# Keeping the row exponentials of half the queries in every step, in an eight-batch attention kernel on one Trainium2 core

## The chip, the cores and the metric

The kernel runs on one core of one Trainium2 chip. A core has five engines that work side by side, each through its own list of instructions in order: TensorE (PE in the profile) multiplies matrices, VectorE (DVE), ScalarE (ACT) and GpSimd (POOL) work on elements, and SyncE (SP) issues transfers. They meet only at semaphores. Sixteen DMA engines move the data that SP and POOL ask for. SBUF has 128 partitions; PSUM, into which TensorE writes, has eight banks of 128 x 512 float32.

The metric is device time in microseconds (us). The kernel before takes 692.85 us, the median of three runs (692.49 to 692.99).

## The reference

The inputs are `x` (8 batches, 512 rows, 512 features), a condition vector per batch, three 512 x 512 weights and three biases, all float32. What has to come out:

```python
def _L0_cond_ref(x, tokens, Wq, bq, Wk, bk, Wv, bv):
    Q = _split_heads(x @ Wq.T + bq)       # 16 heads of 32
    K = _split_heads(x @ Wk.T + bk)
    V = _split_heads(x @ Wv.T + bv)
    tQ = _split_heads(tokens @ Wq.T + bq) # one row per batch
    tK = _split_heads(tokens @ Wk.T + bk)
    cQ = Q + tQ
    cK = K + tK
    scores = jnp.einsum('bhqd,bhkd->bhqk', cQ, cK) / jnp.sqrt(jnp.float32(HEAD_DIM))
    attn = jax.nn.softmax(scores, axis=-1)
    out = jnp.einsum('bhqk,bhkd->bhqd', attn, V)
    return out.transpose(0, 2, 1, 3).reshape(B, S, D_MODEL)
...
x = x + _L0_cond_ref(x, cond_1024[:, None, :], ...)
```

## The kernel before

**Steps.** Eight batches times four groups of four heads make 32 units, t = 0 to 31 (`T = B * G`). The main loop runs t = 1 to 28; each turn is called a step here. A step has four items, i = 0 to 3. The order of the instructions of PE, ACT, DVE and POOL is the order in which the program writes them (`manual_schedule`, L214); SP's DMAs are issued in one queue, in the order in which the scheduler left them, which is nearly the program's.

**What one item does.** `row_max` (L552, L585, L594) makes the scores of 128 queries of the *next* unit against all 512 keys, four heads in four PSUM banks, and takes their maxima on VectorE. `denominators` (L641) runs the exponential over the same banks on ScalarE with the maximum as bias, and keeps the sums; this is the row form, with the query on the partition. The weighted sum with V needs the other form, with the key on the partition. There are two ways to get it.

- *Second scores* (`exponentials`, L693, L696, L707). The maxima are split into three bfloat16 parts on POOL (`split_max`, L655 to L658), turned by a DMA on SP (`turn_max`, L667, the tile `maxT`), and added to a second product of keys and queries: per item four matmuls from `maxT` and four head products of 512 columns, and then four exponentials of 128 x 512 on ScalarE into tiles `e`. The row exponentials themselves are thrown away (they are written back to PSUM).
- *Kept* (`BLOCKED`, t = 3, 7, ..., 27). The row exponentials of all 512 queries are written to SBUF (the tile `blocks`). VectorE turns them in blocks of 32 x 32 (`turn_blocks`, L605, eight of 128 x 1024), and then DMAs exchange the blocks between the four groups of 32 partitions (`swap_blocks`, L625): six pairs of groups, each in three moves (one side to a spare tile `between`, the other side across, the spare tile back), per half of the queries. That is 18 DMAs of 128 KB per half, 36 per unit; of the first half all are on SP, of the second half nine are on SP and nine on POOL. Move 1 waits for move 0 and move 2 for move 1.

**Items and projections.** The four items of a step carry, after the scores, `V` (`weighted`, L716: the weighted sum of unit t - 1, its normalisation on DVE and POOL, and four DMAs of the result on SP, L785) and the products of the next batch's projections of q, k and v, one half of a seven-product scheme per item (`first_products` or `other_products`). Their sums are done on VectorE, except for q and k in blocked steps (`first_by_others`), where ScalarE copies and POOL adds. In a step t that is itself blocked, no item has second scores.

**Other transfers on SP.** Per step four DMAs load the residual `xr` (L188, on which POOL adds the bias at L196), four store the result (L785), one turns `maxT` (L667), and, up to the step in which the last batch is loaded, four load a block of `x` (L170), which VectorE turns (`turn_x`, L351) for the projections of the batch after next.

**Eight banks.** `begin` and `released` (L132, L139) keep a list of banks in the order of their release: an item with second scores uses all eight, an item without uses four for scores and two for the product.

The lines that carry an item are these:

```python
            begin(w)
            if not blocks:
                exponentials(t, i)
            late_first = item in ("v" if blocks else "qkv") and t % 2 == 1
            hold = row_max(*rows, late_first, w)
```

Of the kernel before, what the change touches and what calls it, by code (L numbers as in the profile page):

```python
# [17 lines left out]
def kernel(  # L18
# [38 lines left out]
    nc = tc.nc  # L57
# [13 lines left out]
    BLOCKED = [t for t in range(3, T - 4, G)]  # L71
# [3 lines left out]
    xp = ctx.enter_context(tc.tile_pool(name="xp", bufs=3))  # L75
    xtp = ctx.enter_context(tc.tile_pool(name="xtp", bufs=2))
    qkp = ctx.enter_context(tc.tile_pool(name="qkp", bufs=3))
    ep = ctx.enter_context(tc.tile_pool(name="ep", bufs=10))
# [119 lines left out]
    EB = ctx.enter_context(tc.tile_pool(name="eb", bufs=1))  # L198

    def room(name):  # L200
        return EB.tile([P, HG, NS, HG, P], F32, tag="eb", name=name)

    early = room("early").rearrange("p g c h s -> p (g c) (h s)")
# [126 lines left out]
    def transpose_x(n, pt, leaves=nc.vector.tensor_copy):  # L330

        b, sc = divmod(n, NS)
        if b >= B:
            return
        if sc == 0:
            xT[b] = xtp.tile([P, NC, S], F32, tag="xT", name=f"xT_{b}")
        for cc in range(NC):
            nc.tensor.transpose(
                pt[:, cc * P : (cc + 1) * P], xs[n][:, cc * P : (cc + 1) * P], ident
            )  # L340
        leaves(xT[b][:, :, sc * P : (sc + 1) * P], pt.rearrange("p (c s) -> p c s", c=NC))
        if n:
            load_block(n + 3)

    def turn_x(n):
# [6 lines left out]
        to_load.append(n + 3)  # L352
# [136 lines left out]
    def first_by_others(n, b, u, dens, small, at):  # L489

        one_, two_ = banks(at), banks(at + 1)
        c1, c12, c2, c22 = parts_of(n, b, u)
        dens()
        product(n, b, u, 1, one_[:, :HS])
        product(n, b, u, 6, two_[:, HS:])
        small()
        product(n, b, u, 2, two_[:, :HS], (0,))
        product(n, b, u, 7, one_[:, HS:])
        m1 = c2[:, 0, :]
        nc.scalar.copy(m1, one_[:, :HS])  # L500
        if n == "v":
            nc.scalar.copy(c1[:, 0, :], two_[:, :HS])
            nc.scalar.copy(c12, two_[:, HS:])
            nc.scalar.copy(c22, one_[:, HS:])
        else:
            nc.scalar.copy(c1, halves(two_))
            add = tok[:, "qk".index(n), u * 2 + 1, b : b + 1]
            nc.scalar.activation(c22, one_[:, HS:], AF.Identity, bias=add)
        for o in (c1[:, 0, :], c12):
            nc.gpsimd.tensor_tensor(o, o, m1, ALU.add)  # L510
        nc.gpsimd.tensor_tensor(c22, c22, c12, ALU.add)

    def other_products(n, b, u, dens, small, at):
# [10 lines left out]
        nc.vector.tensor_tensor(c2, halves(one_), twice(c22), ALU.add)  # L524
# [5 lines left out]
    def project_pair(n, b, r, dens, small, at, held):  # L530

        if r % 2:
            held()
        if b >= B:
            dens()
            small()
        elif r % 2:
            other_products(n, b, r // 2, dens, small, at)
        else:
            first_products(n, b, r // 2, dens, small, at, 0, held)  # L540


# [55 lines left out]
    blocked = {}  # L598

    def turn_blocks(t, units):  # L600

        for n in units:
            pr = slice(n % NP * 2, n % NP * 2 + 2)
            e = blocked[t][:, :, n // NP, pr, :].rearrange("p g h s -> p g (h s)")
            nc.vector.transpose(e, e)  # L605

    APART = [(a, g) for a in range(HG) for g in range(a + 1, HG)]
    between = {}

    def swap_blocks(t, half, move):  # L610

        def part(a, g):
            e = blocked[t][a * BL : (a + 1) * BL, g, half * 2 : half * 2 + 2]
            return e.rearrange("p c h s -> p (c h s)")

        if move == 0:
            between[t, half] = [
                ep.tile([P, 2, S], F32, tag="e", name=f"between_{t}_{half}_{i}") for i in range(2)
            ]
        for n, (a, g) in enumerate(APART):  # L620
            at = (n + 2) % HG * BL
            kept = between[t, half][n // HG][at : at + BL].rearrange("p i s -> p (i s)")
            to, of = [(kept, part(a, g)), (part(a, g), part(g, a)), (part(g, a), kept)][move]
            queue = nc.gpsimd if half and n % 2 else nc.sync
            queue.dma_start(to, of)  # L625

    def denominators(t, qc, w=HG):

        if t >= T - 2:
            return  # L630
        for j in range(HG):
            if t in BLOCKED:
                if t not in blocked:
                    blocked[t] = room(f"blocks_{t}")
                to = blocked[t][:, :, qc, j, :].rearrange("p g (c e) -> p g c e", e=BL)
            else:
                to = banks(w + j)
            of = banks(w + j)
            if t in BLOCKED:
# [9 lines left out]
    def split_max(t, on=nc.gpsimd):  # L649

        if t >= T or t in BLOCKED:
            return
# [9 lines left out]
    def turn_max(t):  # L662

        if t >= T or t in BLOCKED:
            return
# [22 lines left out]
    def exponentials(t, kc, at=None):  # L688
# [14 lines left out]
        for pr in range(NP):  # L703
            e = ep.tile([P, 2, S], F32, tag="e", name=f"e_{t}_{kc}_{pr}")
            es[t, kc, pr] = e
# [3 lines left out]
    def times_v(t, kc, pt, chunks=range(NS)):  # L709
        b, g = divmod(t, G)  # L710
        for j in range(HG):
            if t in BLOCKED:
                e = blocked[t][:, :, :, j, kc * BL : (kc + 1) * BL].rearrange("p a c e -> p c a e")
            else:
                e = es[t, kc, j // 2][:, j % 2, :]
# [3 lines left out]
                e,  # L719
                start=(kc == chunks[0]),  # L720
                stop=(kc == chunks[-1]),
            )
# [41 lines left out]
    def weighted(t, pt, pd, between):  # L764
# [4 lines left out]
        for kc in range(NS):  # L769
            times_v(t, kc, pt)  # L770
            if kc == 0:
                spread_sums(apart, pd)
# [200 lines left out]
    def products(t, n, blocks, hold, dens, small):  # L973

        b, r = (t - 1) // G + 1, (t - 1) % G
        if r % 2:
            hold()
            other_products(n, b, r // 2, dens, small, (0, 3))
            released(1, 2, 4, 5, 6, 7, 0, 3)
        elif blocks and n == "v":  # L980
            first_products(n, b, r // 2, dens, small, 5, 4, hold)
            released(6, 7, 0, 1, 2, 3, 5, 4)
        elif blocks:
            hold()
            first_by_others(n, b, r // 2, dens, small, 4)
            released(6, 7, 0, 1, 2, 3, 5, 4)
        else:
            first_products(n, b, r // 2, dens, small, 1, 0, hold)
            released(2, 3, 4, 5, 6, 7, 1, 0)

    TURNED = [((1, 1), (0, 1), (0, 1), (0, 1)), ((0, 0), (0, 1), (0, 1), (0, 1))]
    turned = {}

    def turn_more(t, i, late):

        for u in (t, t + 1):
            if u in BLOCKED:
                n = turned.get(u, 0)
                turned[u] = n + TURNED[t + 1 - u][i][late]
                turn_blocks(u, range(n, turned[u]))  # L1000

    SWAPS = {
        (-1, 2): [(0, 0)],
        (-1, 3): [(0, 1), (0, 2)],
        (0, 3): [(1, 0)],
        (1, 0): [(1, 1)],
        (1, 1): [(1, 2)],
    }

    for t in range(1, T - 3):  # L1010
        b, r = divmod(t, G)
        blocks = t in BLOCKED
        w = 0 if blocks else HG
        items = ["q", "k", "v", "V"] if t - 1 in BLOCKED else ["V", "q", "k", "v"]
        for i, item in enumerate(items):
            rows = (t + 1, i + 1) if i < 3 else (t + 2, 0)
            begin(w)
            if not blocks:
                exponentials(t, i)
            late_first = item in ("v" if blocks else "qkv") and t % 2 == 1  # L1020
            hold = row_max(*rows, late_first, w)

            def held(i=i, hold=hold):
                hold()
                if i == 2:
                    split_max(t + 1)
                    turn_max(t + 1)

            dens = lambda: denominators(*rows, w)
            if item in "qkv":  # L1030
                products(t, item, blocks, held, dens, nothing)
            else:
                held()
                dens()
                if blocks:
                    weighted(t - 1, banks(4), banks(5), nothing)
                    released(6, 7, 0, 1, 2, 3, 5, 4)
                else:
                    weighted(t - 1, banks(0), banks(1), lambda: turn_more(t, i, 0))
                    released(2, 3, 1, 4, 5, 6, 7, 0)  # L1040
            if i == 0 and r == 0:
                turn_x(t + NC + 2)
                turn_x(t + NC + 3)
            if i == 0 and r == 1:
                combine_x(b + 1, 1, nc.gpsimd)
            if i == 1 and r == 0:
                combine_x(b + 1, 0, nc.gpsimd)
            if i == 2 and r == 1:
                turn_x(t + NC + 3)
                turn_x(t + NC + 4)  # L1050
            if i == 3:
                load_blocks()
            if i == 2:
                aparts[t] = masked(t)
            if i == 3:
                load_residual(t + 1)
            turn_more(t, i, 1)
            for u in (t - 1, t, t + 1):
                if u in BLOCKED and (t - u, i) in SWAPS:
                    for swap in SWAPS[t - u, i]:  # L1060
                        swap_blocks(u, *swap)
# [26 lines left out]
    def crossed(t, kc, qc, u=None):  # L1088
# [28 lines left out]
        for pr in (1, 0):  # L1117
            e = ep.tile([P, 2, S], F32, tag="e", name=f"e_{t}_{kc}_{pr}")
# [161 lines left out]
```

## Time and profile before

The profiled execution has a span of 694.0 us, 1.15 us over the median of the three runs, so its rows can be used as they stand.

| What | Value |
|---|---|
| Median of three runs | 692.85 us |
| Profiled execution: span | 694.0 us, 22170 instructions |
| TensorE busy | 677.7 us (98%), 8824 matmuls |
| VectorE busy | 563.5 us (81%) |
| ScalarE busy | 563.6 us (81%) |
| GpSimd busy | 263.9 us (38%) |
| Granted TensorE clock | 0.998 |
| DMA queue of SP and its share of the 16 DMA engines | 54.78 MB, 41.4% |

How to read it: a float32 matmul appears as two matmul records. PE is busy nearly all the time, but its records are pipelined and their ends are modelled, so what a piece of work costs on PE is best read from one start to the next start in the timeline. SP's issuing of DMAs does not count as busy time anywhere; it is seen only in the timeline of SP, where a row gives the start of the first of several equal DMAs, the time until the last of them was issued, and their number. "PEld" is the loading of weights, which overlaps PE.

### The profile page before, as it was taken

The page shows a single profiled execution, that of the slowest core. Times are in us where ns is not written, and L with a number is a line of the kernel's source. Part 1 is how long each engine was busy: PE and PEld are TensorE (multiplying, and loading weights), DVE is VectorE, ACT ScalarE, POOL GpSimd, SP SyncE. Part 2 cuts the span into 40 slices and gives each one's busy share as a digit, 9 for nine tenths or more (in the row PEclk, how much of TensorE's full clock was granted, in tenths as well). Part 3 has the DMA queues.
Part 4 walks back from the last instruction along what each step waited for, and adds up shares of the span by engine and source line. Part 5 has one row for each costly group of instructions (what it writes and reads, how often), then busy time and mean ns, then how long its engine had stood idle before and what let it go on. Part 6 is the DMA issues. An engine that isn't in the chain of part 4 may idle for free.

```text
span 694.0 us, 22170 instructions
## 1 busy us (share of the span) xinstructions
PE 677.7 (98%) x8824; PEld 312.5 (45%) x8824; DVE 563.5 (81%) x878; ACT 563.6 (81%) x1427; POOL 263.9 (38%) x378
## 2 busy tenths in 40 slices
PE   9999999989999999999999999999999999999996
PEld 7444444435445444444445444453544544444331
DVE  4798799857989679886999778996798967987686
ACT  2589887878889888798879888798888988888564
POOL 3722422444236242454315352254423624243361
PEclk9999999999999999999999999999999999999999
DMA  7623236644366443672455624564427622365211
GB/s 188 107 48 55 46 57 145 130 85 70 55 154 152 79 71 69 138 166 48 69 126 116 139 48 74 131 133 108 72 39 154 159 41 41 74 134 146 47 31 31
DMA packets 231674, 65.50 MB, mean 94 GB/s; under 512 B 221834, under 2 KB 222346, under 8 KB 231572
## 3 DMA queue, kind: packets, MB, share of 16 engines
q1 hardware_dynamic: 226788, 54.78, 41.4%
q0 software_dynamic: 3024, 8.26, 4.5%
q8 instruction: 69, 1.13, 0.7%
q10 hardware_dynamic: 1760, 1.05, 0.5%
q14 instruction: 33, 0.27, 0.1%
HBM read 19.75 MB, written 8.39 MB: 41 GB/s over the span
## 4 chain that ended last, share of the span: by engine, by line
PE 83%; DMA 5%; SPq 4%; POOL 4%; issue 2%; ACT 1%; DVE 1%; DVEq 0%; POOLq 0%; ACTq 0%
PE psum L441 35%; PE psum L716 15%; PE psum L585 14%; PE psum L696 10%; PE psum L693 4%; PE psum L384 2%; SPq L785 2%; SPq L188 2%; DMA xr<-in_x_dram 1%; POOL res L782 1%; DMA x<-in_x_dram 1%; POOL res L781 1%; DMA maxT<-split 1%; POOL xr L196 1%; ACT e L707 1%
## 5 line engine op out<-in xcount | busy, mean ns | idle before, releaser
L641 ACT ACTIVATE psum<-psum,nmax 128x512 f32<-128x512 f32 x368 | 244.7, 673 | 28.6 <-DVE nmax L552 21.1
L552 DVE TENSOR_REDUCE nmax<-psum 128x1 f32<-128x512 f32 x298 | 191.3, 683 | 79.1 <-PE psum L585 76.9
L707 ACT ACTIVATE e<-psum 128x512 f32<-128x512 f32 x376 | 194.2, 602 | 66.0 <-PE psum L696 62.5
L585 PE MATMUL psum<-kT,qT 32*128 32x512 f32 x1024 | 143.0, 605 | 0.0
L594 DVE TENSOR_REDUCE nmax<-psum 128x2 f32<-128x1024 f32 x101 | 122.5, 1214 | 1.3 <-PE psum L585 1.3
L781 POOL TENSOR_TENSOR res<-res,recs 128x512 f32<-128x512 f32 x30 | 31.4, 1048 | 174.2 <-DVE res L780 153.6
L696 PE MATMUL psum<-qT,kT 32*128 32x512 f32 x752 | 96.7, 587 | 0.0
L716 PE MATMUL psum<-e,v 128*32 128x512 f32 x800 | 95.3, 597 | 0.0
L196 POOL TENSOR_TENSOR xr<-xr,bvs 128x512 f32<-128x512 f32 x30 | 38.4, 1279 | 145.9 <-DMA xr<-in_x_dram 140.8
L585 PEld LDWEIGHTS psum<-kT,qT 32*128 32x128 f32 x1024 | 60.8, 182 | 52.7 <-issue 23.3
L641 ACT ACTIVATION_READ_ACCUMULATOR psum<-psum,nmax 128x1 f32 x368 | 78.8, 214 | 0.0
L641 ACT ACTIVATE blocks<-psum,nmax 128x512 f32<-128x512 f32 x112 | 76.2, 719 | 0.0
L605 DVE STREAM_TRANSPOSE blocks<-blocks 128x1024 f32<-128x1024 f32 x56 | 68.5, 1224 | 0.0
L441 PE MATMUL psum<-wc_v,xc 128*32 128x256 f32 x768 | 50.2, 379 | 0.0
L441 PE MATMUL psum<-xc,wc_q 128*32 128x256 f32 x720 | 47.1, 379 | 0.0
L441 PE MATMUL psum<-xc,wc_k 128*32 128x256 f32 x720 | 47.1, 379 | 0.0
L716 PEld LDWEIGHTS psum<-e,v 128*32 128x32 f32 x800 | 20.8, 110 | 51.4 <-issue 29.2
L693 PE MATMUL psum<-maxT,onesb 3*128 3x512 bf16 x376 | 37.1, 385 | 2.7 <-DMA maxT<-split 1.9
L782 POOL TENSOR_TENSOR res<-res,xr 128x512 f32<-128x512 f32 x30 | 38.5, 1283 | 2.4
L696 PEld LDWEIGHTS psum<-qT,kT 32*128 32x128 f32 x752 | 37.4, 185 | 1.7
L780 DVE STREAM_TRANSPOSE res<-psum 128x512 f32<-128x512 f32 x28 | 20.1, 717 | 22.0 <-PE psum L716 18.9
L441 PE MATMUL psum<-wT_v,xT 128*32 128x256 f32 x512 | 36.8, 382 | 0.0
(182 smaller groups left out, 895.6 us busy)
## 6 DMA issues: line engine op xcount, KB each, us to landing
between<-blocks SPq DMA_DIRECT2D x63, 128.0 KB, 2.4
blocks<-blocks SPq DMA_DIRECT2D x63, 128.0 KB, 2.4
blocks<-between SPq DMA_DIRECT2D x63, 128.0 KB, 2.9
out_dram<-res SPq DMA_DIRECT2D x122, 64.0 KB, 1.9
xr<-in_x_dram SPq DMA_DIRECT2D x120, 64.0 KB, 2.4
x<-in_x_dram SPq DMA_DIRECT2D x112, 64.0 KB, 2.7
between<-blocks POOLq DMA_DIRECT2D x21, 128.0 KB, 3.5
blocks<-blocks POOLq DMA_DIRECT2D x21, 128.0 KB, 3.2
```

The lines of the kernel that those rows point to most:

```text
L196: nc.gpsimd.tensor_tensor(xr[t], xr[t], bias, ALU.add)
L441: nc.tensor.matmul(pt[r], still[:, r], moving, start=(kc == kcs[0]), stop=(kc == kcs[-1]))
L552: nc.vector.tensor_reduce(nmax[t][:, qc, j : j + 1, 0], pt, AX.X, ALU.max, negate=True)
L585: nc.tensor.matmul(pt, qkT["q", t][r, qc * P : (qc + 1) * P], qkT["k", t][r, :], start=True, stop=True,)
L594: nc.vector.tensor_reduce(nmax[t][:, qc, pr * 2 : pr * 2 + 2, 0], pt, AX.X, ALU.max, negate=True)
L605: nc.vector.transpose(e, e)
L641: nc.scalar.activation(to, of, AF.Exp, bias=nmax[t][:, qc, j, :], accum_out=sums[t][:, qc, j, :],)
L693: nc.tensor.matmul(bank[j], onesb[r, :], maxT[t][r, :], start=True, stop=False)
L696: nc.tensor.matmul(bank[j], qkT["k", t][r, kc * P : (kc + 1) * P], qkT["q", t][r, :], start=False, stop=True,)
L707: nc.scalar.activation(e[:, i, :], bank[pr * 2 + i], AF.Exp)
L716: nc.tensor.matmul(pt[j * HD : (j + 1) * HD, :], vs[b % 2][:, kc, (g * HG + j) * HD : (g * HG + j + 1) * HD], e, start=(kc == chunks[0]), ...
L782: nc.gpsimd.tensor_tensor(y, y, xr.pop(t), ALU.add)
```

## The change

The change spreads the kept form over all of steps 3 to 27 and halves it. `KEPT = range(3, T - 4)` replaces `BLOCKED`: in each of these 25 units the row exponentials of the first two of the four query tiles (256 queries) are kept, turned by four transposes of VectorE, and exchanged by 18 DMAs, all on SP. The other 256 queries get second scores, in two bursts (`exponentials_of_rest`): a burst has four matmuls from `maxT` over 512 columns, eight head products of 256 columns, and four exponentials of 128 x 512; each is an item's worth. So the items 0 and 1 of such a step have no second scores, and the items 2 and 3 have one burst each. The weighted sum is done in two halves of 256 columns, first the half with second scores, then the kept half (`times_v_half`).

With it go other edits:

- All exponentials live in one tile `store` of the same size as the two pools before: three rooms for kept halves, used in turn, four places for the bursts, two for the exchange's spare tile.
- The first halves of the projections are all made by `first_by_others` (two copies of 128 x 512 on ScalarE, two adds on POOL); the second half of v is made by `other_by_others` (two copies on ScalarE, three adds on POOL). VectorE keeps the second halves of q and k. The order of the three projections in a step is given by `MADE`, and `V` is the second item ("PVPP") where the unit before is kept.
- `x` has two buffers in place of three, and one block is loaded per step in place of two every other step.
- The exchange of unit t + 1 is issued at the end of step t, after the load of the residual; that of unit 3 in step 3 after its first item.

```diff
-    BLOCKED = [t for t in range(3, T - 4, G)]
+    KEPT = range(3, T - 4)
+    KQ = NS // 2
...
-    xp = ctx.enter_context(tc.tile_pool(name="xp", bufs=3))
+    xp = ctx.enter_context(tc.tile_pool(name="xp", bufs=2))
...
+    store = EB.tile([P, 18, 2, S], F32, tag="eb", name="store")
+
+    def room(t):
+
+        at = t % 3 * 4
+        return store[:, at : at + 4].rearrange("p g c (h s) -> p g c h s", s=P)
...
+    def first_by_others(n, b, u, dens, at, last):
...
+        product(n, b, u, 1, one_[:, 0])
+        product(n, b, u, 7, one_[:, 1])
+        product(n, b, u, 6, two_[:, 1])
+        product(n, b, u, 2, two_[:, 0], (0,))
         dens()
...
+        nc.scalar.copy(c2, one_)
+        nc.scalar.copy(c1, two_)
+        last()
+        nc.gpsimd.tensor_tensor(c1, c1, twice(c2[:, 0, :]), ALU.add)
         nc.gpsimd.tensor_tensor(c22, c22, c12, ALU.add)
...
+    def other_by_others(n, b, u, dens, small, at):
...
+        nc.scalar.copy(m45, halves(one_))
+        nc.scalar.copy(m23, halves(two_))
+        nc.gpsimd.tensor_tensor(c12, m45[:, 1, :], c12, ALU.add)
+        nc.gpsimd.tensor_tensor(c2, m45, twice(c22), ALU.add)
+        nc.gpsimd.tensor_tensor(c1, m23, c1, ALU.add)
...
+    def turn_kept(t, n):
+
+        pr = slice(n % NP * 2, n % NP * 2 + 2)
+        e = kept[t][:, :, n // NP, pr, :].rearrange("p g h s -> p g (h s)")
+        nc.vector.transpose(e, e)
...
+    between = store[:, 16:18]
+
+    def swap_kept(t, move):
 
         def part(a, g):
-            e = blocked[t][a * BL : (a + 1) * BL, g, half * 2 : half * 2 + 2]
-            return e.rearrange("p c h s -> p (c h s)")
...
+            return kept[t][a * BL : (a + 1) * BL, g].rearrange("p c h s -> p (c h s)")
+
         for n, (a, g) in enumerate(APART):
             at = (n + 2) % HG * BL
...
-            queue = nc.gpsimd if half and n % 2 else nc.sync
-            queue.dma_start(to, of)
+            aside = between[at : at + BL, n // HG].rearrange("p i s -> p (i s)")
+            to, of = [(aside, part(a, g)), (part(a, g), part(g, a)), (part(g, a), aside)][move]
+            nc.sync.dma_start(to, of)
...
+    def exponentials_of_rest(t, half):
+
+        bank = [banks(i) for i in range(HG)]
+        rest = slice(KQ * P, S)
+        for j in range(HG):
+            r = slice(j * HD, j * HD + 3)
+            nc.tensor.matmul(
+                bank[j],
+                onesb[r, :],
+                maxT[t][r, rest].unsqueeze(1).broadcast_to([3, 2, HS]),
+                start=True,
+                stop=False,
+            )
+        for i in range(2):
+            kc = half * 2 + i
+            for j in range(HG):
+                r = slice(j * HD, (j + 1) * HD)
+                nc.tensor.matmul(
+                    bank[j][:, i * HS : (i + 1) * HS],
+                    qkT["k", t][r, kc * P : (kc + 1) * P],
+                    qkT["q", t][r, rest],
+                    start=False,
+                    stop=(i == 1),
+                )
+        for pr in range(NP):
+            e = es[t, half, pr] = store[:, 12 + half * 2 + pr]
+            for i in range(2):
+                nc.scalar.activation(e[:, i, :], bank[pr * 2 + i], AF.Exp)
...
+        if t in KEPT:
+            for kc in range(NS):
+                times_v_half(t, kc, 1, pt)
+            spread_sums(apart, pd)
+            for kc in range(NS):
+                times_v_half(t, kc, 0, pt)
...
+    def bursts(s, i):
+
+        if s not in KEPT:
+            return [(s, i)]
+        return [(s, i - 2)] if i >= 2 else []
+
+    TURNED = {(0, 1): 1, (1, 1): 1, (2, 0): 1, (3, 1): 1}
...
+        items = "PVPP" if t - 1 in KEPT else "VPPP"
...
             if i == 3:
                 load_residual(t + 1)
...
+            if i == 3 and t in KEPT and t + 1 in KEPT:
+                for move in range(3):
+                    swap_kept(t + 1, move)
+            if (t, i) == (KEPT[0], 0):
+                for move in range(3):
+                    swap_kept(t, move)
```

258 lines of the change are left out of this document (119 added, 139 removed).

## The prediction

> **What bounds the kernel now.** I read the page's busy times first, then the page's chain, then windows over steps 3 to 27, and last the timelines of PE and SP inside these steps.
>
> ```profile
> span 694.0 us, 22170 instructions
> PE 677.7 (98%) x8824; PEld 312.5 (45%) x8824; DVE 563.5 (81%) x878; ACT 563.6 (81%) x1427; POOL 263.9 (38%) x378
> ...
> PE 83%; DMA 5%; SPq 4%; POOL 4%; issue 2%; ACT 1%; DVE 1%; DVEq 0%; POOLq 0%; ACTq 0%
> ```
>
> ```profile
> 108.90:622.30 513.40, 506.68 (x6868) 230.79 (x6864) 427.45 (x656) 438.83 (x1132) 199.81 (x295) 1.00 0.50 101
> 193.70:211.10 17.40, 17.40 (x244) 7.40 (x240) 15.37 (x22) 13.81 (x40) 7.84 (x13) 1.00 0.67 143
> 211.10:232.80 21.70, 21.70 (x300) 10.34 (x300) 17.91 (x29) 19.89 (x52) 9.41 (x17) 1.00 0.66 149
> ```
>
> The windows' columns are length, busy us of PE, PEld, DVE, ACT and POOL, clock, DMA share, GB/s. The first row is steps 3 to 27: 513.4 us for 25 steps. The second is step 7 (kept), the third step 8. PE is busy throughout, and 83% of the chain is PE: TensorE bounds the kernel. The 9% of DMA and SPq in the chain are the first hint that transfers are not all hidden.
>
> What an item costs on PE is read from start to start:
>
> ```profile
> 193.75 1.14 PE L585 MATMUL psum<-kT,qT 32*128 32x512 f32 x8
> ...
> 198.45 1.14 PE L585 MATMUL psum<-kT,qT 32*128 32x512 f32 x8
> ...
> 202.68 1.14 PE L585 MATMUL psum<-kT,qT 32*128 32x512 f32 x8
> ...
> 204.64 1.05 PE L441 MATMUL psum<-xc,wc_k 128*32 128x256 f32 x16
> 205.50 0.61 PE L441 MATMUL psum<-xT,wT_k 128*32 128x256 f32 x8
> ...
> 206.91 1.14 PE L585 MATMUL psum<-kT,qT 32*128 32x512 f32 x8
> ...
> 211.37 1.03 PE L696 MATMUL psum<-qT,kT 32*128 32x512 f32 x8
> 212.23 1.02 PE L585 MATMUL psum<-kT,qT 32*128 32x512 f32 x8
> ...
> 216.35 0.40 PE L693 MATMUL psum<-maxT,onesb 3*128 3x512 bf16 x4
> ...
> 221.56 0.39 PE L693 MATMUL psum<-maxT,onesb 3*128 3x512 bf16 x4
> ```
>
> A projection item without second scores takes 206.91 - 202.68 = 4.23 us, the V item without them 198.45 - 193.75 = 4.70, a projection item with them 221.56 - 216.35 = 5.21. A burst is worth 0.98. Four heads of 512 columns take 212.23 - 211.37 = 0.86; two groups of four with 256 columns take 205.50 - 204.64 = 0.86 as well, so halving the columns costs nothing by itself.
>
> Now SP, which counts as busy nowhere:
>
> ```profile
> 105.86 5.03 SPq L625 DMA_DIRECT2D between<-blocks  x6
> 110.99 3.70 SPq L625 DMA_DIRECT2D blocks<-blocks  x6
> 114.73 4.56 SPq L625 DMA_DIRECT2D blocks<-between  x6
> 119.39 2.19 SPq L785 DMA_DIRECT2D out_dram<-res  x4
> 122.95 1.21 SPq L667 DMA_TRANSPOSE maxT<-split  x1
> 124.21 3.74 SPq L188 DMA_DIRECT2D xr<-in_x_dram  x4
> ...
> 138.41 4.93 SPq L170 DMA_DIRECT2D x<-in_x_dram  x8
> ```
>
> ```profile
> 601.84 4.57 SPq L625 DMA_DIRECT2D between<-blocks  x6
> 606.72 3.69 SPq L625 DMA_DIRECT2D blocks<-blocks  x6
> 610.46 5.16 SPq L625 DMA_DIRECT2D blocks<-between  x6
> 615.72 2.21 SPq L785 DMA_DIRECT2D out_dram<-res  x4
> 618.95 2.10 SPq L667 DMA_TRANSPOSE maxT<-split  x1
> 621.09 2.17 SPq L188 DMA_DIRECT2D xr<-in_x_dram  x4
> ```
>
> These are the first and the last of seven exchanges of 18 DMAs, of exactly the size that the change issues in each of 25 steps. From the first issue to the end of the last they take 12.3 to 14.2 us, 13.1 in the mean, all of it SP's own time. The next rows say why some are longer:
>
> ```profile
> L625 SPq DMA_DIRECT2D between<-blocks x63: 507/589/2140, 105.9 to 625.7; - x63
> ...
> blocks<-between SPq DMA_DIRECT2D x63, 128.0 KB, 2.9
> ...
> maxT<-split SPq DMA_TRANSPOSE x22, 2.5
> ```
>
> The issue of one takes 0.59 us in the median and now and then 1.2 to 2.1. Such long issues fall about 9 us apart. The page's queue of instruction loads has 69 packets in the span, one per 10 us, and the long issues lie on those (packets at 106.5 and 116.5 us, long issues of the first exchange at 106.5 and 116.6):
>
> ```profile
> q8 instruction: 69, 1.13, 0.7%
> ```
>
> **The change part by part.** *TensorE.* Steps 3 to 27 had 18 x 4 = 72 bursts and get 50. By the items above 22 x 0.98 = 21.6 us go. The weighted sum in halves and the bursts in 256 columns cost 0 by the equal 0.86; its cover is that weights load beside the matmuls (7.40 us of PEld in 17.40), and if that were gone it would cost the difference between 1.05 (the row's own length) and 0.86 per pair of groups: 25 x 12 groups are 150 pairs, 0.19 x 150 = 28 us at most. I take 0, since the 256-column row is the nearest. A step then needs 4.23 + 4.70 + 2 x 5.21 = 19.35 us of PE, 25 steps 484. The 513.4 of before also hold waits: seven kept steps of 17.4 and 18 of 21.3 (3 x 5.21 + 5.68, V being 0.47 longer) make 505; 8 us are waits.
>
> *VectorE and ScalarE.*
>
> ```profile
> L605 DVE STREAM_TRANSPOSE blocks<-blocks 128x1024 f32<-128x1024 f32 x56 | 68.5, 1224 | 0.0
> ...
> L707 ACT ACTIVATE e<-psum 128x512 f32<-128x512 f32 x376 | 194.2, 602 | 66.0 <-PE psum L696 62.5
> ...
> L506 ACT COPY kT<-psum 128x512 f32<-128x512 f32 x7 | 4.2, 605 | 0.0
> L476 DVE COPY v<-psum 128x256 f32<-128x256 f32 x14 | 5.8, 414 | 0.0
> ```
>
> The transposes go from 56 to 100: +44 x 1.22 = +54 us on VectorE. It loses the first halves of the projections and v's second halves: 126 operations of 256 columns (0.41) and, net, 28 of 512 (about 0.6, half of 1.22 for 1024), 69 us. That leaves (427 + 54 - 69)/25 = 16.5 us a step, under 19.35. ScalarE loses 88 exponentials at 194.2/376 = 0.52 (-46) and gains 98 copies of 512 columns at up to 0.6 less 28 short ones of about 0.4 (+48): it stays near 438.8/25 = 17.6. POOL gains 70 adds of 512 columns (1.28 each, by a row below) and loses the issue of 63 DMAs: 199.8/25 = 8.0 a step become at most 11.6. All three stay under PE, and lie beside it. Costed at 0; if an item's ScalarE work runs over PE's (an item with a burst and two copies needs some 5.7 for 5.21), the cost is 0.5 x 25 = 12 us at most.
>
> *SP.* Here the cost stands. In each of steps 3 to 26 SP issues an exchange (13.1), a block of x (4.93/2 = 2.4), a result (2.2), maxT (1.3) and the residual (2.3, with 2.2 and 3.7 in the rows), with 0.1 between groups, 0.5 in all: 21.8 us. That is more than PE's 19.35, so SP falls behind by 2.4 us a step. Ends: without any long issue 3 x 3.69 + 2.2 + 1.2 + 2.2 + 2.4 and 0.4 between are 19.5; the first exchange with its neighbours adds up to 13.4 + 2.2 + 1.2 + 3.7 + 2.4 = 23.0. I take 21.8, from the mean of the seven, since the instruction loads go on and an SP that never rests meets every one.
>
> Who waits: all of it is one queue in order. The exchange is followed by x, the result, and then by maxT of the unit after, without which the bursts of that unit (L693) can't begin; behind maxT stands xr, on which POOL's adds wait (L196). The weighted sum's kept half waits for the last move, which lands 2.9 after its issue. What is late next is maxT, about 2 us per step. That such a wait reaches PE is seen once already, in step 4 behind two exchanges:
>
> ```profile
> 146.96 1.06 PE L716 MATMUL psum<-blocks,v 128*32 128x512 f32 x8 [1.75 <-DMA blocks<-between]
> ```
>
> *The sum*, along SP, to maxT of unit 28, which step 28 needs in its first item:
>
> ```profile
> 115.77 1.28 POOL L782 TENSOR_TENSOR res<-res,xr 128x512 f32<-128x512 f32 x1
> ...
> 622.32 0.40 PE L693 MATMUL psum<-maxT,onesb 3*128 3x512 bf16 x4
> ```
>
> In SP's order the result of unit 2 stands behind the first DMA of unit 3's exchange; it is ready at 115.8 + 1.3 = 117.1. From there 2.2 (result), 1.2 (rest of x), 12.4 (17 of the exchange) and 3.8 (maxT, xr): unit 4's exchange starts at 136.7. Units 4 to 22 are 19 x 21.8 = 414.2, units 23 to 26, with no x left, 4 x 19.4 = 77.6, and unit 27's exchange, a result and maxT to its landing 13.1 + 2.2 + 0.3 + 2.5 = 18.1: 646.6. Before, that burst started at 622.3. The rest is as before: 694.0 + 24.3 = 718.3, and, since the profiled execution stands 1.15 over the median, 717 us. PE, with 484 us from 108.9, would be there at 593.
>
> **The rivals.** *SP keeps up; TensorE decides (faster).* If a step's issues take 19.4 us or less, the 21.6 us of bursts go, and up to 8 us of waits: 663 to 671. For it: the last move of one exchange was issued while earlier ones were in flight, so 3.7 for six may be bound by data and not by issuing, and idle gaps could swallow the long issues. Against it: no exchange of the seven took less than 12.3. The Trainium skill has a rule that speaks for this rival: "DMA: Bandwidth & Descriptors", section "Issuing engines are not separate DMA queues", says that the sequencer's time to initiate a DMA is usually small relative to the DMA itself. By that page's fabric ceiling of 435 GB/s ("Where 436 GB/s comes from") a 128 KB move is an estimated 0.3 us, 18 of them 5.4, and a step on SP 14, so SP would have room. The trace differs: 0.59 of issue each, 18 in 12.3 or more.
>
> *Between.* A step on SP of 19.5 to 20.7: break-even is where 24.3/23 = 1.06 us a step are missing from 21.8, at 20.7. 664 to 691.
>
> *It waits on itself (slower still).* If PE's wait for the last move and SP's wait for PE's later items come one behind the other, the 1.75 above recurs in 25 steps, +44: 761. Against it: by the sum each thing that SP issues is ready by its turn (split of maxT some 6 us into an item that began with the last maxT).
>
> **How the numbers follow.** SP bounds the steps: 0.70, with 700 to 742 (21.0 to 22.9 a step). SP keeps up: 0.15. Between: 0.07. Within 0.2% of before, which is about what a measurement can tell here: 0.03. It waits on itself: 0.05. Faster 0.22, same 0.03, slower 0.75. The point is SP's, 717. The range leaves out the first rival and the last, 0.20: 680 (20.2 a step) to 742.
>
> **What would show it.** Right: SP's timeline has no gap from 120 to 640 us, and a step (from one first transpose of `store` to the next) takes about 21.8 us up to unit 22 and 19.4 to 20 after; PE is busy under 93%, with 40 us or more of waits on maxT and on the exchange. An exchange still takes 13 us. Wrong: gaps on SP in each step, steps of 19.4 (first rival), or steps of over 23 with SP waiting for semaphores (last). What would make the prediction wrong first is the 13.1: the same DMAs taking 11 or 15 us when one exchange follows another without a rest.

## The result, and the profile after

The changed kernel takes 728.01 us, the median of four runs (724.80 to 731.27), against 692.92 us before (four runs): a ratio of 1.048 with a 95% interval from 1.0427 to 1.0532. It is slower, by 35 us. Its profiled execution, the slowest of the four, took 731.27 us and has a span of 729.3 us. In all runs here the time of an execution is about 2 us (1.7 to 2.4) more than its span, so the 694.0 us of span before belong to an execution of an estimated 696 us, about 3 us over its median and not 1.15; below, spans are compared with spans.

The page of the kernel after (span, busy times, the chain, SP's largest group of DMAs):

```profile
span 729.3 us, 24078 instructions
PE 682.2 (94%) x9760; PEld 345.6 (47%) x9760; DVE 555.7 (76%) x740; ACT 564.3 (77%) x1409; POOL 335.1 (46%) x427
...
PE 68%; SPq 16%; DMA 5%; POOL 5%; DVE 3%; issue 2%; ACT 1%; DVEq 0%; POOLq 0%
...
store<-store SPq DMA_DIRECT2D x450, 128.0 KB, 2.4
```

The page's DMA queues (SP's is the first, the second loads instructions; packets, MB, share of the 16 engines):

```profile
q1 hardware_dynamic: 243124, 89.93, 60.8%
q8 instruction: 77, 1.26, 0.8%
```

TensorE's busy share falls from 98% to 94%, and SP's queue rises in the chain from 4% to 16%. The window over steps 3 to 27 of the kernel after, columns as in the prediction:

```profile
112.14:658.08 545.94, 505.72 (x7773) 260.44 (x7770) 429.54 (x544) 435.38 (x1106) 263.41 (x338) 0.97 0.72 149
```

These 25 steps took 513.4 us before and take 545.9 now: 32.5 of the 35.3 us by which the span grew. Of the 545.9, PE is idle for 40.2. VectorE and ScalarE have as much to do as before, POOL 64 us more, and all three have room. SP's timeline in the kernel after, at the first exchanges, at unit 23, and at the last one:

```profile
120.69 1.95 SPq L833 DMA_DIRECT2D out_dram<-res  x4
122.69 1.03 SPq L170 DMA_DIRECT2D x<-in_x_dram  x2
123.76 11.68 SPq L628 DMA_DIRECT2D store<-store  x17
135.48 2.42 SPq L668 DMA_TRANSPOSE maxT<-split  x1
137.94 2.18 SPq L188 DMA_DIRECT2D xr<-in_x_dram  x4
140.24 14.13 SPq L628 DMA_DIRECT2D store<-store  x18
154.42 2.23 SPq L170 DMA_DIRECT2D x<-in_x_dram  x4
156.76 2.04 SPq L833 DMA_DIRECT2D out_dram<-res  x4
158.90 2.40 SPq L668 DMA_TRANSPOSE maxT<-split  x1
161.35 2.17 SPq L188 DMA_DIRECT2D xr<-in_x_dram  x4
...
559.27 13.27 SPq L628 DMA_DIRECT2D store<-store  x18
...
638.77 14.36 SPq L628 DMA_DIRECT2D store<-store  x18
653.23 2.21 SPq L833 DMA_DIRECT2D out_dram<-res  x4
655.54 1.22 SPq L668 DMA_TRANSPOSE maxT<-split  x1
```

Each row of the first block begins where the one before it ends, within 0.12 us. From 120.7 to 659.0 us SP has no gap between two issues longer than 0.42 us. From unit 4's exchange to unit 23's there are 19 cycles in 419.0 us, 22.05 each; from unit 23's to unit 27's four in 79.5, 19.9 each. An exchange takes 12.9 us in the mean (11.3 to 14.4).

What PE waits for in the kernel after (us in total, times, longest), with the first row of another engine's waits that leads to it:

```profile
POOL xr L196 <- DMA xr<-in_x_dram: 152.0, 24, 9.8
PE psum L451 <- POOL xc L381: 24.7, 6, 4.9
PE psum L715 <- DMA maxT<-split: 12.5, 9, 3.0
PE psum L694 <- DMA maxT<-split: 2.3, 1, 2.3
```

The largest wait isn't on SP's transfers themselves. The timelines of POOL and PE, kernel after, step 5, show how it arises:

```profile
165.76 1.26 POOL L196 TENSOR_TENSOR xr<-xr,bvs 128x512 f32<-128x512 f32 x1 [9.31 <-DMA xr<-in_x_dram]
166.98 1.26 POOL L380 TENSOR_TENSOR xc<-xT 128x512 f32<-128x512 f32 x1
168.20 1.26 POOL L381 TENSOR_TENSOR xc<-xT,xc 128x512 f32<-128x512 f32 x1
```

```profile
162.53 0.40 PE L715 MATMUL psum<-maxT,onesb 3*128 3x512 bf16 x4 [1.64 <-DMA maxT<-split]
...
169.52 1.94 PE L451 MATMUL psum<-xc,wT_q 128*32 128x256 f32 x16 [4.87 <-POOL xc L381]
171.23 1.93 PE L451 MATMUL psum<-xc,wc_q 128*32 128x256 f32 x16
172.93 1.04 PE L451 MATMUL psum<-xT,wT_q 128*32 128x256 f32 x8
```

SP issues the residual late, POOL stands in order in front of its bias (L196) for 9.31 us, and behind it wait two adds (L380, L381) without which the next batch's projection can't begin. This occurs in every fourth step, six times.

### The profile page after: what moved, and what is told of

Same layout as the page of the kernel before. It is cut to its first block, busy times and chain, and to the rows that moved or that the text cites. A ratio compares the mean times of both kernels' runs of the same rounds, so it can differ in the third digit from the quotient of the medians.

```text
span 729.3 us, 24078 instructions
## 1 busy us (share of the span) xinstructions
PE 682.2 (94%) x9760; PEld 345.6 (47%) x9760; DVE 555.7 (76%) x740; ACT 564.3 (77%) x1409; POOL 335.1 (46%) x427
## 3 DMA queue, kind: packets, MB, share of 16 engines
q1 hardware_dynamic: 243124, 89.93, 60.8%
## 4 chain that ended last, share of the span: by engine, by line
PE 68%; SPq 16%; DMA 5%; POOL 5%; DVE 3%; issue 2%; ACT 1%; DVEq 0%; POOLq 0%
PE psum L451 31%; PE psum L595 14%; SPq L628 7%; PE psum L757 6%; PE psum L726 4%; PE psum L741 3%; SPq L833 3%; PE psum L697 3%; DMA xr<-in_x_dram 2%; SPq L188 2%; SPq L170 2%; PE psum L394 2%; SPq L668 2%; PE psum L715 1%; DMA maxT<-split 1%
## 5 line engine op out<-in xcount | busy, mean ns | idle before, releaser
L562 DVE TENSOR_REDUCE nmax<-psum 128x1 f32<-128x512 f32 x242 | 155.9, 686 | 102.6 <-PE psum L595 101.3
L642 ACT ACTIVATE psum<-psum,nmax 128x512 f32<-128x512 f32 x280 | 185.7, 670 | 17.9 <-DVE nmax L604 9.4
L736 ACT ACTIVATE store<-psum 128x512 f32<-128x512 f32 x200 | 103.3, 604 | 84.4 <-PE psum L726 84.4
L604 DVE TENSOR_REDUCE nmax<-psum 128x2 f32<-128x1024 f32 x129 | 156.7, 1215 | 2.8 <-PE psum L595 2.8
L642 ACT ACTIVATE store<-psum,nmax 128x512 f32<-128x512 f32 x200 | 136.2, 692 | 12.1 <-DVE nmax L604 7.1
L614 DVE STREAM_TRANSPOSE store<-store 128x1024 f32<-128x1024 f32 x100 | 122.5, 1226 | 0.0
L196 POOL TENSOR_TENSOR xr<-xr,bvs 128x512 f32<-128x512 f32 x30 | 38.3, 1275 | 163.2 <-DMA xr<-in_x_dram 152.0
L757 PE MATMUL psum<-store,v 128*32 128x256 f32 x1600 | 93.3, 381 | 0.0
L757 PEld LDWEIGHTS psum<-store,v 128*32 128x32 f32 x1600 | 46.9, 110 | 45.0 <-ACT store L642 17.4
L707 ACT ACTIVATE store<-psum 128x512 f32<-128x512 f32 x88 | 45.5, 608 | 14.8 <-PE psum L697 11.5
L726 PE MATMUL psum<-qT,kT 32*128 32x256 f32 x800 | 53.1, 382 | 0.0
L451 PE MATMUL psum<-xc,wT_q 128*32 128x256 f32 x240 | 20.3, 465 | 24.7 <-POOL xc L381 24.7
L642 ACT ACTIVATION_READ_ACCUMULATOR store<-psum,nmax 128x1 f32 x200 | 41.5, 207 | 0.0
```

The lines of the kernel that those rows point to most:

```text
L451: nc.tensor.matmul(pt[r], still[:, r], moving, start=(kc == kcs[0]), stop=(kc == kcs[-1]))
L562: nc.vector.tensor_reduce(nmax[t][:, qc, j : j + 1, 0], pt, AX.X, ALU.max, negate=True)
L604: nc.vector.tensor_reduce(nmax[t][:, qc, pr * 2 : pr * 2 + 2, 0], pt, AX.X, ALU.max, negate=True)
L642: nc.scalar.activation(to, of, AF.Exp, bias=nmax[t][:, qc, j, :], accum_out=sums[t][:, qc, j, :],)
L707: nc.scalar.activation(e[:, i, :], bank[pr * 2 + i], AF.Exp)
L726: nc.tensor.matmul(bank[j][:, i * HS : (i + 1) * HS], qkT["k", t][r, kc * P : (kc + 1) * P], qkT["q", t][r, rest], start=False, stop=(i == 1),
```

## The experiments

The prediction's theory is that SP's issuing bounds steps 3 to 27. The rivals after the result were the 16 DMA engines (their share is now 60.8% in SP's queue), POOL's place for the bias, and TensorE itself.

**Without the exchange.** SP's 18 DMAs go, so the kept half is weighted with blocks that were not exchanged; everything else stays.

```diff
-            if i == 3 and t in KEPT and t + 1 in KEPT:
-                for move in range(3):
-                    swap_kept(t + 1, move)
-            if (t, i) == (KEPT[0], 0):
-                for move in range(3):
-                    swap_kept(t, move)
```

> The changed kernel without the 18 exchange DMAs of each step (so the kept half is weighted with blocks that were turned but not exchanged; everything else stays). Theory, SP's issuing bounds steps 3 to 27: a step then costs SP about 9 us, PE decides with 19.4 us a step, and the time is 663 to 672 us. Rival, the other edits of the change (projections on ScalarE and POOL, weighted sum in halves) cost time of their own: it stays above 680 us. If it stays at 720 or more, neither the exchange nor SP has to do with it.

672.50 us (672.30 to 672.69), 0.9715 of before (0.9690 to 0.9740). The window of steps 4 to 26 in this run:

```profile
132.35:581.06 448.71, 448.71 (x7180) 235.48 (x7177) 398.04 (x505) 398.75 (x1014) 244.97 (x311) 1.00 0.28 47
```

PE is never idle: 23 steps of 19.51 us, against the 19.35 that the prediction worked out. So the 55 us between this run and the kernel after hang on the exchange; VectorE, ScalarE and POOL, all with their added work, do not bound these steps. It does not yet tell whether SP or the data cost them.

**Half the bytes, and half the rows.** Two runs keep the 18 DMAs and halve what each moves, so half of the exchange is left out: once half the bytes of each of the 32 rows, once half of the rows.

```diff
-            return kept[t][a * BL : (a + 1) * BL, g].rearrange("p c h s -> p (c h s)")
+            return kept[t][a * BL : (a + 1) * BL, g, 0].rearrange("p h s -> p (h s)")
...
-            aside = between[at : at + BL, n // HG].rearrange("p i s -> p (i s)")
+            aside = between[at : at + BL, n // HG, 0]
```

> The changed kernel with each of the 18 exchange DMAs moving half the bytes (64 KB: the blocks of one of the two kept query tiles; the other tile's blocks stay where they were turned). The number of DMAs is the same. If an issue costs what it costs for each DMA, whatever its bytes: the pitch falls only to that of the other 64 KB DMAs on SP (0.53 in place of 0.63 to 0.67 us), 450 x 0.1 to 0.14 = 45 to 63 us less, 665 to 685 us, with an exchange of 10 to 11 us. If the bytes set the pitch (the DMA engines back up into the queue): 0.32 us each, an exchange of 6 to 7 us, PE bound, 663 to 670 us. The exchange's own length in SP's timeline tells the two apart better than the time.

```diff
-            return kept[t][a * BL : (a + 1) * BL, g].rearrange("p c h s -> p (c h s)")
+            rows = slice(a * BL, a * BL + BL // 2)
+            return kept[t][rows, g].rearrange("p c h s -> p (c h s)")
...
-            aside = between[at : at + BL, n // HG].rearrange("p i s -> p (i s)")
+            aside = between[at : at + BL // 2, n // HG].rearrange("p i s -> p (i s)")
```

> Each of the 18 DMAs of an exchange moves only the first 16 of its 32 partitions, each with all its bytes (64 KB in place of 128); so half of the exchange is left out. This halves the rows of a DMA, where the run with half the bytes kept the 32 rows and halved each. If the 0.59 us of issue are paid per DMA, or by the bytes' other half of the story is right that nothing in a DMA's size matters, the exchange stays at about 12 us and the time near that run's 716.7 us: 712 to 722. If the issue is paid per row, it falls to some 0.3 to 0.4, an exchange to 6 to 7 us, a step on SP to about 16, TensorE bounds, and the time is 668 to 674, as without any exchange (672.5).

Half the bytes: 716.73 us (715.55 to 717.90), where both theories had expected 663 to 685. Half the rows: 714.74 us (713.74 to 715.75), as the first of its two cases said. The issue of an exchange's DMA (ns, min/median/max) in the kernel after, with half the bytes, and with half the rows:

```profile
L628 SPq DMA_DIRECT2D store<-store x450: 507/589/2293, 115.3 to 652.5; - x150
```

```profile
L628 SPq DMA_DIRECT2D store<-store x450: 507/588/2199, 114.9 to 639.7; - x150
```

```profile
L629 SPq DMA_DIRECT2D store<-store x450: 507/587/1804, 115.1 to 635.2; - x150
```

The median stays at 0.59 us: in these three sizes the price of an issue is per DMA. The expectation of the first run failed because it let the pitch fall with the bytes. SP stays the late one in both runs, with no gap longer than 0.43 us from 120 to 640 us.

Only the mean issue of an exchange's DMA falls, from 0.666 to 0.630 and 0.634, by the long issues: 35 of more than 0.8 us in the kernel after, 1.69 us each in the mean, then 29 of 1.42 and 34 of 1.32. Over the usual 0.58 that is 39 us against 24 and 25. All of SP's issues together take 564.1 us in the profiled execution of the kernel after, then 551.2 and 546.1; they fall by 13 and 18 us, and so do the spans (729.3, then 716.1 and 711.8). Why the long ones cost less with half the data stays open; it isn't the data alone that sets their length, since in the fastest version below, with all of it, 46 take 1.33 us each, 35 us over the usual.

That the DMA engines' throughput is the bound falls: half the data gave back a fifth to a quarter of the 55 us that taking the exchange away gave.

**The results issued by POOL.** Four DMAs of each step go to another queue; the data is the same.

```diff
-            nc.sync.dma_start(spread(out[b], g * P + h * BL), y[h * BL : (h + 1) * BL])
+            nc.gpsimd.dma_start(spread(out[b], g * P + h * BL), y[h * BL : (h + 1) * BL])
```

> The changed kernel with one line moved: the four DMAs that store a result are issued by POOL, right behind POOL's own last add, in place of SP. Same bytes, same DMA engines. Theory, SP's issuing bounds: SP's step falls by 4 x 0.59 = 2.4 us, from 22.0 to 19.7, close to PE's 19.4; 24 such steps give 728 - 57 = 671 us, 668 to 680 us. Rival, the 16 DMA engines are the bound (they are 70% busy in the steps): the same bytes in the same time, 722 to 732 us. Rival, POOL becomes the bound with the added issues: slower than 728.

683.33 us (681.35 to 685.74), 0.9877 of before (0.9843 to 0.9912); expected were 668 to 680. The kernel is now 1.2% faster than before: 4 of SP's 31 DMAs a step were worth 45 us. SP's cycle is 19.7 us (from unit 4's exchange at 135.6 to unit 27's at 589.2). It lies so close to PE's 19.5 that single steps still wait; the largest PE item, in step 17, takes 9.57 in place of 5.2, again for L196 and `xc`.

The same edit in the kernel *before*, as a counter-test:

> The kernel before, with the four result DMAs of a step issued by POOL in place of SP. Theory: SP there has some 53 us of issues in four steps of 82 us, so it bounds nothing on the whole, and only late exchanges behind the results cost: 688 to 693 us. If the time falls by more than 5 us, SP's queue already held up the kernel before, and the gain of the other variants is not the change's.

693.77 us, a ratio of 1.0000 (0.9987 to 1.0013). Moving the results gained nothing there. In the kernel before, SP issues nothing in 226 of the 540 us from 120 to 660 (gaps of more than 0.3 us), against gaps of 0.42 at most in the kernel after: it is the change that made SP the bound.

**The bias later.** POOL adds the bias after the next step's first item; SP's list is the same.

```diff
+        if later:
+            return lambda: nc.gpsimd.tensor_tensor(xr[t], xr[t], bias, ALU.add)
         nc.gpsimd.tensor_tensor(xr[t], xr[t], bias, ALU.add)
...
-                load_residual(t + 1)
+                add_bias = load_residual(t + 1, True)
+            if i == 0 and t > 1:
+                add_bias()
```

> The changed kernel with POOL's add of the bias to the residual (L196, which waits for the residual's DMA) put behind the first item of the next step, so that POOL's work for the next batch's projection (xc) no longer stands behind a late DMA. SP's list is the same. Theory, SP's issuing bounds and PE's long waits on xc are only the place where SP's lag shows: the waits move to maxT and to the exchange, 722 to 732 us. Rival, the chain residual, POOL, xc, PE is the cause: six waits of about 5 us with slow matmuls behind each go, 36 to 50 us, 680 to 695 us.

723.16 us (722.87 to 723.46). All the waits on `xc` are gone, and others stand in their place:

```profile
PE psum L717 <- DMA maxT<-split: 31.5, 15, 3.5
PE psum L696 <- DMA maxT<-split: 7.5, 1, 7.5
```

39.0 us on maxT, against 39.5 on `xc` and maxT together in the kernel after. The place of a wait changed, its sum did not, since SP was the late one. SP's cycles are 21.8 (19 in 414.5 us) and 19.5 us here.

**Every second exchange DMA issued by POOL.** This splits the expensive group itself over two queues.

```diff
-            nc.sync.dma_start(to, of)
+            (nc.gpsimd if n % 2 else nc.sync).dma_start(to, of)
```

> The changed kernel with every second DMA of the exchange (9 of 18) issued by POOL, nothing else moved: same bytes, same 16 DMA engines. Theory, SP's issuing bounds: SP's step falls by 9 x 0.67 = 6 us to 16, and the time to 672 to 685 us, unless POOL, which waits in its own list between the moves (three landings of about 3.5 us beside 11.6 us of work and 4.5 of issues), gets late with the maxima: then up to 700. Rival, the DMA engines' work is the bound: 722 to 732 us.

816.50 us (815.42 to 818.95), 1.177 of before, far above the expected 672 to 700. The waits of this run:

```profile
POOL store L628 <- DMA store<-store: 96.8, 94, 2.9
...
PE psum L451 <- POOL xc L381: 60.8, 6, 12.1
...
DVE qT L524 <- POOL qT L512: 49.5, 7, 8.9
...
PE psum L595 <- DVE qT L476: 42.0, 7, 8.2
```

```profile
SPq L833 <- POOL split L656: 194.6, 24, 10.8
SPq L628 <- DMA store<-store: 57.8, 82, 2.4
```

The second move of a pair waits for the first to land. Issued by SP in groups of six, that wait is hidden behind the other five pairs. With three pairs left on POOL it isn't: POOL waits 96.8 us for the moves, and behind that stand its adds for `xc` (60.8 us of PE's waits) and for the projections, for which VectorE and then PE wait (49.5 and 42.0). SP now waits as well, behind the same late POOL and for the moves. The prediction's last rival, priced at 761, was of this kind, a queue that waits on itself, though between SP and PE; here it goes through POOL and costs 88 us over the kernel after, twice the 44 of that rival.

**Results and residuals issued by POOL,** with the bias later:

```diff
-                nc.sync.dma_start(
+                (nc.gpsimd if later else nc.sync).dma_start(
                     xr[t][h * BL : (h + 1) * BL], spread(x[b], g * P + h * BL)
```

> The changed kernel with the four result DMAs and the four residual DMAs of a step issued by POOL, and the bias add put behind the first item of the next step, so that POOL doesn't wait for its own load. Theory, SP's issuing bounds: SP's step falls from 22.0 by 2 x 2.4 us to 17.2, clearly under PE's 19.5, all waits on maxT and on the exchange go, and the time is that of the kernel without any exchange: 672 us, 670 to 677. If the exchange itself (its latency of some 16 us, or its bytes beside the others) held PE up, a part stays: 680 us or more.

678.93 us (678.56 to 681.02), 0.9792 of before (0.9768 to 0.9817). Steps 4 to 26 take as long as without an exchange. The 7.6 us by which the span is longer than in that run lie at the edges: 1.6 in step 3, 2.7 in a wait of step 28's burst for maxT, and the rest behind it.

**VectorE's projections outside steps 3 to 27,** in addition: there all four items have a burst, and ScalarE's copies come on top of it.

```diff
+        if plain and product == "first":
+            first_products(n, b, u, dens, nothing, 1)
+            by_vector.add((n, b, u))
+            last()
+            return released(2, 3, 4, 5, 6, 7, 1, 0)
...
-            if n == "v":
+            if n == "v" and not plain:
...
-                products((t - 1) // G + 1, *next(made), alone, dens, last)
+                products((t - 1) // G + 1, *next(made), alone, dens, last, t not in KEPT)
```

> As the last but one (results and residual on POOL), and the projections of steps 1, 2 and 28, where every item has second scores, made by VectorE as in the kernel before. Theory, the two copies per projection cost time only where an item has a burst and copies together and ScalarE's work (4.75 + 1.0 us) passes PE's 5.2: steps 1, 2 and 28 lose the 5 us that they took longer, 667 us, 664 to 670. If the copies cost nothing there, it stays at that kernel's time.

678.00 us (675.89 to 678.57). Step 3 begins 1.6 us earlier (three items of steps 1 and 2 took 5.36, 6.38 and 5.65 us, in the kernel after 6.06, 6.52 and 6.07); the rest of the expected gain did not come. POOL's timeline in this run shows one reason, four DMAs issued just ahead of the split of unit 28's maxima:

```profile
596.23 2.59 POOL L835 DMA_DIRECT2D out_dram<-res  x4 [0.30 <-POOL res L832]
598.81 0.27 POOL L658 CAST split<-nmax 128x16 bf16<-128x16 f32 x1
```

**POOL as issuer inside only.** The last results and residuals return to SP, which is idle there:

```diff
-                (nc.gpsimd if later else nc.sync).dma_start(
+                (nc.gpsimd if later and t < T - 5 else nc.sync).dma_start(
...
-            nc.gpsimd.dma_start(spread(out[b], g * P + h * BL), y[h * BL : (h + 1) * BL])
+            (nc.gpsimd if t < T - 6 else nc.sync).dma_start(
+                spread(out[b], g * P + h * BL), y[h * BL : (h + 1) * BL]
+            )
```

> The fastest version so far (results and residuals issued by POOL, the bias added later, VectorE's projections outside steps 3 to 27; 678.0 us), but POOL issues only the results of units up to 25 and the residuals of units up to 26; the rest go to SP again, which is idle there. In that version POOL issued the result of unit 26 for 2.6 us just ahead of the split of unit 28's maxima (the burst of step 28 waited 2.4 us), and a late result ahead of the masked sums (a wait of 1.5 us). If these are what is lost at the end, both waits go: 674, between 672 and 676. If step 28 is late for another reason (its maxima, VectorE), 677 to 678.

672.78 us (672.21 to 675.24), 0.9717 of before (0.9689 to 0.9746): the fastest version, 20 us under the kernel before and 55 under the change as made. Its busy times and its window of steps 4 to 26:

```profile
span 671.0 us, 24060 instructions
PE 662.4 (99%) x9760; PEld 338.9 (51%) x9760; DVE 560.6 (84%) x758; ACT 559.3 (83%) x1401; POOL 454.7 (68%) x617
```

```profile
131.74:580.39 448.65, 448.65 (x7180) 235.63 (x7176) 397.44 (x504) 398.20 (x1012) 363.83 (x495) 1.00 0.76 169
```

Steps 4 to 26 take 448.65 us, against 448.71 without any exchange. The same 18 DMAs of 128 KB are in it, at a DMA share of 0.76 where the kernel after had 0.72, so the DMA engines had room there. The exchange is wholly hidden once SP issues 23 DMAs a step in place of 31. Of the two waits at the end the one on the masked sums is gone; that of step 28's burst fell from 2.4 to 1.7 us.

## Why the prediction was right

Its mechanism holds: SP's queue bounds the steps. Taking away its DMAs (672.5 us) or moving four (683.3) or eight (672.8) of them to another issuer takes the bound away, and making each DMA of the exchange smaller (717 and 715) does not. The time was 11 us above the predicted 717, inside the range. By the prediction's own steps, in the profiled execution (729.3 us of span, where the sum had 718.3):

| Term of the sum | Predicted | Measured | Miss |
|---|---|---|---|
| Unit 4's exchange starts | 136.7 | 140.24 | +3.5 |
| Units 4 to 22 | 19 x 21.8 = 414.2 | 419.0 | +4.8 |
| Units 23 to 26 | 4 x 19.4 = 77.6 | 79.5 | +1.9 |
| Unit 27 to step 28's burst | 18.1 | 19.3 (638.77 to 658.08) | +1.2 |
| From there to the end | 71.7 | 71.2 | -0.5 |

- *The start* was late on PE's side, not by SP: from the result of unit 2 (120.69) to unit 4's exchange it takes 19.55 us, the 19.6 predicted. The prediction costed ScalarE's copies at 0, with 12 us at most; its own remark that an item with a burst and two copies needs 5.7 us was the better one for steps 1 and 2, whose projection items took 6.06 and 6.07 in place of 5.21 and whose V item took 6.52 in place of 5.68. Step 3 began at 112.14, not 108.9; 2.5 of these 3.2 us lie in these three items, 0.6 ahead of step 1. VectorE in ScalarE's place gave back 1.6; what the V item lost isn't separated. Inside steps 3 to 27, where two items of four have no burst, the 0 was right.
- *The cycle* was sized from seven exchanges that stood alone. In the 19 cycles the exchange itself, in a row with others, took 12.85 us in the mean, 0.25 less than the 13.1 predicted; what the prediction feared for it, 11 or 15 us, did not come. What stands between the exchanges took 9.2 where the sum had 8.7: the block of `x` 2.65 (2.4 predicted), the result 2.32 (2.2), maxT 1.39 (1.3), the residual 2.38 (2.3), the gaps between groups 0.45 (0.5). The two misses partly cancel, so the 22.05 against 21.8 looks nearer than its terms are.
- *PE's step* was right (19.35 predicted, 19.51 in the run without an exchange), so the 0 for the halves of the weighted sum and the 21.6 us off the bursts were near too: without the exchange the 25 steps take 488.4 us, 484 predicted, 513.4 before. VectorE's work was put too low: it takes 429.5/25 = 17.2 us a step, 16.5 predicted, and that is still under PE's.
- *What is late next* was wrong in its place. The prediction named maxT, about 2 us in each step. Only 14.8 us are there; 24.7 come in six lumps by the residual, POOL's bias and `xc`. The prediction had named xr and L196 as waiting behind maxT, but not what POOL does after them. Moving the bias shows that this decided where the time was lost, and only some 5 us of how much.
- *Signs.* SP without a gap from 120 to 640 us: so. PE busy under 93%: 92.6% in steps 3 to 27 (505.72 of 545.94), 94% of the whole span. An exchange of 13 us: 12.9. At least 40 us of waits on maxT and on the exchange: not so, 14.8 on maxT and none on the exchange; with the 24.7 on `xc` they are 39.5.
- *The rule that spoke for the first rival* ("DMA: Bandwidth & Descriptors", section "Issuing engines are not separate DMA queues", of the Trainium skill: time to initiate a DMA is usually small relative to the DMA). For one DMA the trace agrees, 0.59 us of issue against 2.4 to landing. For the kernel it decided wrongly, since landings overlap (18 of 2.4 us in an exchange of 12.9) and issues of one queue do not: 450 x 0.666 us are 300 of SP's time. The same sentence says that more issuers save just that time, and moving eight DMAs, with the two small edits beside it, saved 55 us.

## What to carry to other kernels

Count the DMAs of each issuing queue in a step and multiply them by the issue time in the trace: the queue is an engine with a busy time of its own, though the page shows none, and here 31 DMAs a step were 22 us against 19.5 of TensorE. Independent DMAs moved to an engine with time to spare took that bound away. Fewer and larger ones should, by the equal price of an issue, but no run here tried that. A chain of DMAs that wait for each other stays on one queue, with enough others in between. Where a wait moves when its nearest cause is mended and its sum stays, the late one is further back.

## What the runs showed of the hardware

- *The issue of an exchange's DMA costs the same in three sizes:* 0.587 to 0.589 us in the median for 32 rows of 4 KB, 32 of 2 KB and 16 of 4 KB. The loads of 64 KB from the input take 0.49 (L170, L188).
- *After the idle 4.87 us PE ran at half rate:* sixteen matmul records of 256 columns took 1.71 us (169.52 to 171.23) and the next sixteen 1.70 (to 172.93), in place of 0.86, and the window of these 3.4 us shows the granted clock at 0.50. The same followed a wait of only 1.75 us for maxT in step 16:

```profile
169.50:172.90 3.40, 3.38 (x32) 1.58 (x36) 0.00 (x0) 0.00 (x0) 3.24 (x4) 0.50 0.85 195
...
404.84 0.40 PE L715 MATMUL psum<-maxT,onesb 3*128 3x512 bf16 x4 [1.75 <-DMA maxT<-split]
...
405.90:409.30 3.40, 3.40 (x28) 1.16 (x27) 1.42 (x3) 2.76 (x7) 1.79 (x2) 0.50 0.78 180
```

  After the waits of 1.64 and 1.73 us it did not; of the waits of PE from 1.75 to 4.87 us in the kernel after, each was followed by 3.4 or 6.8 us at half rate. The Trainium skill, "TensorE: Matmul & The Clock Gate", Part 1, says that the clock halves after an idle window of about 3.4 us and comes back after as much work. The trace agrees on the half rate and on the 3.4 us that it lasts at least, but not on the idle time: six of the ten waits that it followed were shorter, 1.75 to 3.18 us. In the run with results and residuals on POOL a wait of 2.67 us was not followed by it, so no fixed length of a wait comes out of these runs. In steps 3 to 27 this adds 17 us to PE's busy time (505.7, 488.4 without an exchange). It cost nothing in the end, by this reading, because SP had no gap in which to wait for PE; no run separates it.
- *Long issues on SP (1.2 to 2.3 us)* go on at the rate that the prediction read from the instruction loads, of which the page now shows 77: of SP's 58 issues of more than 1.1 us (maxT's apart), 56 lie within 0.3 us of such a packet. With half the data in the exchange they cost less (above). No run here took these loads away, so the cause is argued, not shown.
